# Softmax sums of an attention layer: from TensorE's matmuls to VectorE's turned blocks and transfers

## The chip, the core and the metric

The kernel runs on one core of a Trainium2 chip. The time is the device time in microseconds of one execution. A core has five engines that work side by side, each through its own queue in order: TensorE (PE, matmuls; PEld is its weight load), VectorE (DVE), ScalarE (ACT), GpSimd (POOL) and SyncE (SP), which here only issues transfers (DMAs). TensorE writes to PSUM, eight banks of 128 x 512 f32; the other engines move data between PSUM and SBUF; DRAM is reached by transfers.

## The reference

Two layers follow each other on x of 4 x 1024 x 512 (f32), each with an attention branch s and a feed-forward branch g, and x + s * silu(g) as output. The change touches the attention of layer 1 alone, with 16 heads of 32:

```python
q, k, v = (proj(wq), proj(wk), proj(wv))     # x @ w.T, split into 16 heads of 32
q, k = apply_rope(q, k, sin, cos)
att = jnp.einsum('bhqd,bhkd->bhqk', q, k) * (1.0 / math.sqrt(HD))
att = jax.nn.softmax(att, axis=-1)
y = jnp.einsum('bhqk,bhkd->bhqd', att, v)
y = y.transpose(0, 2, 1, 3).reshape(b, t, c)
return y @ wo.T
```

The softmax divides by the sum over the 1024 keys of the exps. The kernel divides late: it multiplies the undivided y by one over that sum.

## The kernel before, in words

Layer 0 comes first, then layer 1's attention, then layer 1's feed-forward. The attention is cut into 32 units (batch b, group g of four heads, half qh of the queries: 512 queries), in the list `units`; `nu` is 32. Each unit has TB = 8 steps, and one loop over s counts the steps of all units. A step s does two things, for units some way apart:

- for unit s // 8 it finds maxima. `top` (L998) makes scores `sq` of 128 queries with 512 keys for two heads at a time, twice a step, and VectorE reads each `sq` once for its maxima `mx` (L1011). At the unit's last step the maxima are joined, turned (`turn_max`, L1013) and sent by way of DRAM (`turned_d`) to rows `mT`;
- for e = s - 12 (LAG is 12) it weighs. `expo` (L1030) makes the scores `sk` of 128 keys with the unit's 512 queries for four heads, subtracts the maxima by another small matmul (L1043), and ScalarE writes the exps to `pT` (L1048). `weigh` (L1052) multiplies the previous step's `pT` with v into `y`, over the eight steps of a unit. So unit u's exps fall into steps 8u + 12 to 8u + 19.

`exps` (L1063) also adds the eight `pT` of a unit up into `part`, 128 keys x 4 heads x 512 queries: the first add L1077, six more L1079, all on GpSimd. What is left is the sum over the 128 partitions. `total` (L944) does that on TensorE: four matmuls with a matrix of ones (L947) write `z`, where the sum of each query stands in 32 rows, which is how `y` is laid out. It does so at s % 8 == 6 for the unit zu = (s - 6) // 8 - 2, three steps behind that unit's last exp. `divide` (L952) copies `z` from PSUM to `zs` (ScalarE, L956), takes reciprocals (VectorE, four times 128 x 128, L960) and multiplies on GpSimd (L961, `yT` <- `yr`, `zs`). Units 30 and 31 have no full `part`: their sums are built by `total` step by step. When a batch's four groups are divided, `soon` names the step at which its output projection (`wo_out`) joins the work below.

Between these parts, TensorE does slices of longer chains, four `advance` a step: the projections wk, wq and wv of the next group of heads (`heads_in`; their results get the rotary part on VectorE, L919, by transfers `rr` <- `raw`, L916, and on GpSimd, L920 and L921) and the output projection. In a step with `total`, the first of the four comes behind it.

PSUM: `ring` has three tiles of two banks, taken in turn by two `sq` and two `sk` a step, so the second `sk` of a step takes the tile of the step's first `sq`, and the next step's first `sq` the tile of the second; `y` and `acc1` have one bank each, and `acc1` serves `z` and the chains. In SBUF `pT` has three buffers, `part` two, `yr` and `zs` one.

TensorE's instructions run as the code writes them (`manual_schedule` for that engine). The order on the other engines is chosen when the kernel is built, by a scheduler that places an instruction where it reckons that its operands are ready; only what stands in `keep_in_program_order` keeps its place. An engine takes its queue in order: an instruction that waits holds up all behind it.

Of the kernel before, what the change touches and what calls it, by code (L numbers as in the profile page):

```python
# [12 lines left out]
F32 = mybir.dt.float32  # L13
# [3 lines left out]
ALU = mybir.AluOpType  # L17
AX = mybir.AxisListType

P = 128  # L20
B, N, D = 4, 1024, 512
NT = B * N
H, HD = 16, 32
# [12 lines left out]
def kernel(ctx, tc, ins, out):  # L36
    nc = tc.nc
# [3 lines left out]
    dram = ctx.enter_context(tc.tile_pool(name="dram", bufs=1, space=bass.MemoryType.DRAM))  # L41
# [47 lines left out]
    def shared_tile(tag, name):  # L89
        return w0.tile([P, KD, D], F32, tag=tag, name=name)  # L90
# [155 lines left out]
    with ExitStack() as es:  # L246
# [4 lines left out]
        p2 = es.enter_context(tc.tile_pool(name="a0", bufs=2, reuse_waits="tile"))  # L251
# [318 lines left out]
    with ExitStack() as es:  # L570
# [3 lines left out]
        p2 = es.enter_context(tc.tile_pool(name="f0", bufs=2, reuse_waits="tile"))  # L574
# [126 lines left out]
        for g in range(NH0 * NBLK + 2 + 2 * TPB):  # L701
            blk, c = divmod(g, NH0)
            if g == NH0 * NBLK:

                for n in ("wk", "wq", "wv"):
# [3 lines left out]
                            out=W[n], in_=ins[n + "T"].rearrange("(k p) n -> p k n", p=P)  # L709
# [8 lines left out]
            for i in range(TPB):  # L718
                q = g - 2 - 2 * i
# [95 lines left out]
    with ExitStack() as es:  # L815
        wp = es.enter_context(tc.tile_pool(name="a1c", bufs=1, reuse_waits="tile"))
        p2 = es.enter_context(tc.tile_pool(name="a1", bufs=2, reuse_waits="tile"))

        def ring(name):
            return pp.tile([P, 2, 512], F32, tag="ring", name=name, bufs=3)  # L820

        def acc1(name):
            return pp.tile([P, 512], F32, tag="acc1", name=name)

        TB = N // P
# [4 lines left out]
        def load1(b):  # L830
            xnTs[b] = xpair(f"xnT1_{b}")
            for h in range(2):
                load = nc.sync.dma_start(
                    out=xnTs[b][h],
                    in_=xnT_d[b].rearrange("k p n -> p k n")[:, :, h * BLK : (h + 1) * BLK],
                )
                if b:
                    tc.keep_in_program_order(load)
# [7 lines left out]
        turned_d = [  # L846
            dram.tile([8, 512], F32, tag=f"turned{i}", name=f"turned_d{i}") for i in range(2)
        ]

        partner = []  # L850
        for i in range(2):
# [92 lines left out]
        def total(z, part, kb, n):  # L944

            for h in range(4):
                nc.tensor.matmul(  # L947
                    z[h * HD : (h + 1) * HD, :], lhsT=ones[:, :HD], rhs=part[:, h, :],
                    start=(kb == 0), stop=(kb == n - 1),
                )  # L950

        def divide(u, yr, z):  # L952

            b, g, qh = u
            zs = p2.tile([P, 512], F32, tag="zs", name=f"zs_{b}_{g}_{qh}", bufs=1)
            nc.scalar.copy(zs, z)  # L956
            yT = p2.tile([P, 512], F32, tag=f"yT{qh}", name=f"yT_{b}_{g}_{qh}", bufs=5 + qh)
            for c in range(TPB):
                cols = slice(c * P, (c + 1) * P)
                nc.vector.reciprocal(zs[:, cols], zs[:, cols])  # L960
            nc.gpsimd.tensor_tensor(yT, yr, zs, ALU.mult)  # L961
            yTs[b][g, qh] = yT
# [29 lines left out]
        def advance(parts):  # L992
            nonlocal chain
            for _ in range(parts):
                if chain is not None:
                    next(chain)
# [88 lines left out]
        units = [(b, g, qh) for b in range(B) for g in range(4) for qh in range(2)]  # L1085
        nu, LAG = len(units), TB + 4
        yTs = {b: {} for b in range(B)}
# [18 lines left out]
            tc.tile_pool(name="psuma", bufs=1, space=PSUM, reuse_waits="tile")  # L1106
        )
        must, spare = deque(), deque()
        mx, mTs, pTs, ys, parts, lates, soon = {}, {}, {}, {}, {}, {}, {}
        for s in range(TB * nu + LAG + 1):  # L1110

            e = s - LAG
            if s % (2 * TB) == 0 and s < TB * nu:

                assert not must
                n = s // (2 * TB) + 1
                if n < 4 * B:  # L1120
                    b, g = divmod(n, 4)

                    two = (nc.sync, nc.gpsimd) if s == 0 else (nc.sync, nc.sync)
                    must.extend(
                        heads_in(
                            b, g, acc1, {(w, h): two for w in ("wk", "wq") for h in range(2)}
                        )
                    )
                    if g == 3 and b + 1 < B:
                        load1(b + 1)  # L1130
                left = 2
            if s in soon and s < TB * nu:
                spare.extend(wo_out(*soon.pop(s), acc1))
            if s % 2 == 0:

                chain = None
                if spare and left and s < TB * nu:
                    chain = spare.popleft()
                    left -= 1
                elif must:  # L1140
                    chain = must.popleft()
            if s == 2 * TB:
                W["wo"] = shared_tile("wo", "wo")
                tc.keep_in_program_order(
                    nc.sync.dma_start(
                        out=W["wo"], in_=ins["woT"].rearrange("(k p) n -> p k n", p=P)
                    )
                )
            if s % 4 == 0 and s // 4 < TPB:
                lates[s + 2] = s // 4, late(s // 4)  # L1150
            if s < TB * nu:
                u, j = divmod(s, TB)
                if j == 0:
                    mx[u] = p2.tile([P, TPB, 4, 2], F32, tag="mx", name=f"mx_{u}")
                for pair in range(2):
                    top(u, j, pair, mx[u])
                if j == TB - 1:
                    m2 = twice[u % 2][:, :, :8].rearrange("p q (h c) -> p q h c", c=2)

                    w = p2.tile([P, TPB, 4, 2], F32, tag="m1", name=f"m1_{u}")  # L1160
                    nc.vector.tensor_reduce(
                        w[:, :, :, 0], mx.pop(u), AX.X, ALU.max, negate=True
                    )
                    for out, sign in ((w[:, :, :, 1], -1.0), (m2[:, :, :, 0], 1.0)):
                        nc.scalar.activation(
                            out.bitcast(F32R), w[:, :, :, 0], AF.Copy, scale=sign
                        )
                    nc.vector.tensor_reduce(m2[:, :, :, 1], w, AX.X, ALU.add)
            late_exp = s >= TB * nu
            if late_exp:  # L1170
                exps(e)
            if 1 <= e <= TB * nu:
                u, kb = divmod(e - 1, TB)
                if kb == 0:
                    ys[u] = pp.tile([P, 512], F32, tag="y", name=f"y_{u}")
                weigh(u, kb, pTs[e - 1], ys[u])
                if u >= nu - 2:

                    if kb == 0:
                        z_last = acc1(f"z_{u}")  # L1180
                    if u < nu - 1 or kb < TB // 2:
                        total(z_last, pTs[e - 1], kb, TB)
                pTs.pop(e - 2, None)
                if kb == TB - 1:
                    yr = p2.tile([P, 512], F32, tag="yr", name=f"yr_{u}", bufs=1)
                    nc.scalar.copy(yr, ys[u])
                    ys[u] = yr
                    if u == nu - 2:
                        divide(units[u], ys.pop(u), z_last)
                        soon[s] = units[u][0], units[u][2], yTs[B - 1]  # L1190
            held = 0
            zu = (s - 6) // TB - 2
            if s % TB == 0 and 0 < s <= TB * nu:
                turn_max(s // TB - 1)
            if s % TB == 6 and 0 <= zu < nu - 2:
                z = ring(f"z_{zu}")[:, 0, :] if zu == nu - 3 else acc1(f"z_{zu}")
                total(z, parts.pop(zu), 0, 1)
                divide(units[zu], ys.pop(zu), z)
                b, g, qh = units[zu]
                if g == 3:  # L1200
                    soon[s + 4] = b, qh, yTs[b]
            elif s in lates:
                late_turn(*lates.pop(s))
            else:
                held = 1
                advance(1)
            if not late_exp:
                exps(e)
            advance(4 - held)
            if TB * nu - 12 <= s < TB * nu:  # L1210

                nxt = weight(raw1, w0, True)
                if loaded:
                    loaded()
                loaded = nxt
                if s == TB * nu - 1:
                    loaded()

        soon = [*soon.values()]
# [307 lines left out]
```

## Time and profile before

| | |
|---|---|
| median of 3 runs (lowest, highest) | 3093.51 us (3091.0, 3093.84) |
| the profiled execution | 3092.08 us |
| its span, first to last instruction | 3090.2 us |
| TensorE's mean granted clock | 0.996 of full speed |
| `mx` L1011, VectorE, 128 x 1024 | 512 times, 1218 ns each |
| `pT` L1048, ScalarE, 128 x 1024 | 512 times, 1020 ns each |
| `part` L1077 and L1079, GpSimd, 128 x 2048 | 210 times, 4.5 us each |
| `z` L947, TensorE | 33.5 us with `part`, 12.5 us with `pT` |
| `zs` L960, VectorE, 128 x 128 | 128 times, 908 ns each |
| `yT` L961, GpSimd, 128 x 512 | 32 times, 1273 ns each |

How to read the profile: the page gives the busy time of each engine, then the span in 40 slices, in tenths. In groups a line reads: line of the kernel, engine, operation, output <- input, shapes, count | busy time and mean ns | idle time just before, and what ended it. In a timeline a line begins with its start and its length in us, and brackets show how long the engine stood idle before and what released it. SPq is SyncE's queue, where issuing a transfer takes the time shown; its data land later.

### The profile page before, as it was taken

To read this page: it belongs to the slowest core of one execution; us is meant where nothing else is said; L and a number is where in the kernel's file an instruction comes from. 1 tells how busy PE (TensorE), PEld (TensorE's weight loads), DVE (VectorE), ACT (ScalarE), POOL (GpSimd) and SP (SyncE) were. 2 spreads that over 40 slices of the span, in tenths; PEclk is the share of its full clock that TensorE was granted. 3 is DMA by queue.
4 is the path that set the end of the run, shared out by engine and by line. 5 is a ranking of instruction groups with operands and counts; after the bars stand their busy time and mean duration, and the time that the engine had idled before them with its cause. 6 is when DMAs were issued, how large, how long until landed. Compare 5 with 4: busy or idle time off the path is not lost.

```text
span 3090.2 us, 61139 instructions
## 1 busy us (share of the span) xinstructions
PE 3038.3 (98%) x25985; PEld 1730.5 (56%) x25985; DVE 1788.3 (58%) x2569; ACT 1173.7 (38%) x1708; POOL 1557.9 (50%) x742
## 2 busy tenths in 40 slices
PE   9999999999999998999999999999999999999998
PEld 5555555578788873333334444333434436888886
DVE  4444555467777776555555555555555544566655
ACT  3111111145556542444444444444444454333332
POOL 1221212234443444888888988888988940001001
PEclk9999999999999999999999999999999999999999
DMA  4222232323223231100001000100000014222111
GB/s 137 86 86 86 86 86 72 127 96 100 95 92 110 96 129 52 36 9 9 9 18 42 16 10 15 43 16 14 10 18 15 13 46 152 82 69 75 58 52 56
DMA packets 113787, 186.81 MB, mean 60 GB/s; under 512 B 19809, under 2 KB 33633, under 8 KB 113377
## 3 DMA queue, kind: packets, MB, share of 16 engines
q1 hardware_dynamic: 106096, 161.30, 17.3%
q0 software_dynamic: 7280, 21.39, 1.9%
q8 instruction: 205, 3.36, 0.5%
q14 instruction: 78, 0.63, 0.1%
q10 hardware_dynamic: 128, 0.13, 0.0%
HBM read 115.11 MB, written 59.26 MB: 56 GB/s over the span
## 4 chain that ended last, share of the span: by engine, by line
PE 57%; DVE 1%; ACT 1%; POOL 1%; issue 0%; SPq 0%; DMA 0%; ACTq 0%; POOLq 0%; DVEq 0%
PE sk L1037 9%; PE sq L1007 8%; PE y L1056 8%; PE gate L1260 5%; PE up L1260 5%; PE dn L1282 5%; PE wo L862 4%; PE v1ps L862 3%; PE wk L862 3%; PE wq L862 3%; PE sk L1043 2%; PE z L947 1%; ACT pT L1048 1%; DVE zs L960 1%; POOL part L1079 0%; DVE mx L1011 0%
## 5 line engine op out<-in xcount | busy, mean ns | idle before, releaser
L1011 DVE TENSOR_REDUCE mx<-sq 128x2 f32<-128x1024 f32 x512 | 604.2, 1218 | 434.8 <-PE sq L1007 434.0
L1079 POOL TENSOR_TENSOR part<-part,pT 128x2048 f32<-128x2048 f32 x180 | 817.8, 4543 | 17.3 <-ACT pT L1048 8.9
L1048 ACT ACTIVATE pT<-sk 128x1024 f32<-128x1024 f32 x512 | 495.6, 1020 | 557.3 <-PE sk L1043 520.1
L1007 PE MATMUL sq<-wkT,wqT 32*128 32x512 f32 x2048 | 321.0, 639 | 10.0 <-ACT pT L1048 7.0
L1037 PE MATMUL sk<-wqT,wkT 32*128 32x512 f32 x2048 | 322.8, 641 | 0.8 <-DVE mx L1011 0.5
L1056 PE MATMUL y<-pT,v 128*32 128x512 f32 x2048 | 275.5, 608 | 0.1
L1304 POOL TENSOR_TENSOR th<-th,x 128x512 f32<-128x512 f32 x31 | 40.1, 1293 | 458.0 <-DVE th L1303 379.0
L646 PE MATMUL pj<-wpj,hp 128*128 128x512 f32 x1024 | 262.0, 396 | 4.0 <-DVE hp L606 4.0
L593 PE MATMUL fc<-xp,wfc 128*128 128x512 f32 x1024 | 259.0, 395 | 3.6 <-ACT h L598 2.8
L614 POOL TENSOR_TENSOR sums<-sums,h 128x512 f32<-128x512 f32 x112 | 163.1, 1456 | 195.0 <-ACT h L598 189.7
L1043 PE MATMUL sk<-mT,onesr 2*128 2x512 f32 x1024 | 235.7, 788 | 0.0
L382 PE MATMUL qk<-xnT,wqkv 128*128 128x512 f32 x512 | 228.7, 600 | 0.7 <-ACT xnT L156 0.7
L646 PEld LDWEIGHTS pj<-wpj,hp 128*128 128x128 f32 x1024 | 191.2, 188 | 51.9 <-DVE hp L606 10.5
L593 PEld LDWEIGHTS fc<-xp,wfc 128*128 128x128 f32 x1024 | 189.4, 188 | 47.2 <-ACT h L598 6.0
L606 DVE TENSOR_TENSOR hp<-h,hp 128x512 fp32r<-128x512 f32 x128 | 128.2, 1001 | 85.2 <-ACT hp L603 85.2
L1260 PE MATMUL gate<-xp,wf 128*128 128x512 f32 x704 | 174.2, 390 | 0.0
L1260 PE MATMUL up<-xp,wf 128*128 128x512 f32 x704 | 173.9, 389 | 0.0
L1037 PEld LDWEIGHTS sk<-wqT,wkT 32*128 32x128 f32 x2048 | 96.2, 184 | 138.3 <-issue 117.2
L1282 PE MATMUL dn<-wf,hp 128*128 128x512 f32 x704 | 173.6, 390 | 0.0
L1077 POOL TENSOR_TENSOR part<-pT,pT 128x2048 f32<-128x2048 f32 x30 | 136.4, 4548 | 72.1 <-ACT pT L1048 72.0
L1007 PEld LDWEIGHTS sq<-wkT,wqT 32*128 32x128 f32 x2048 | 89.9, 184 | 122.7 <-issue 85.5
L382 PEld LDWEIGHTS qk<-xnT,wqkv 128*128 128x128 f32 x512 | 95.0, 191 | 111.8 <-issue 104.5
(230 smaller groups left out, 4359.3 us busy)
## 6 DMA issues: line engine op xcount, KB each, us to landing
s<-s SPq DMA_DIRECT2D x96, 256.0 KB
xp<-xp_d SPq DMA_DIRECT2D x16, 1024.0 KB
x<-x SPq DMA_DIRECT2D x36, 256.0 KB
x<-in_x SPq DMA_DIRECT2D x32, 256.0 KB
raw_fc<-in_w_fcT SPq DMA_DIRECT2D x32, 256.0 KB
xp_d<-hi POOLq DMA_DIRECT2D x32, 256.0 KB, 2.7
xp_d<-xnT POOLq DMA_DIRECT2D x32, 256.0 KB, 2.9
x0r<-in_x SPq DMA_DIRECT2D x32, 256.0 KB
```

Source lines behind the costliest of these rows:

```text
L382: nc.tensor.matmul(a, lhsT=wqkv[k][:, c0 : c0 + P], rhs=xnTs[blk][:, k, :], start=(k == 0), stop=(k == KD - 1),)
L593: nc.tensor.matmul(a, lhsT=wfc[k][:, c * P : (c + 1) * P], rhs=xp[n][:, k, :].bitcast(F32R), start=(k == 0 and n == 0), stop=(k == KD - 1 ...
L646: nc.tensor.matmul(ds[i], lhsT=hparts[blk, c][n][:, i * P : (i + 1) * P], rhs=wpj[c], start=(c == 0 and n == 0), stop=(c == NH0 - 1 and n ...
L862: nc.tensor.matmul(out[r0 : r0 + HD, :], lhsT=lhsT[:, r0 : r0 + HD], rhs=rhs, start=start, stop=stop,)
L1007: nc.tensor.matmul(sq[:, hh, :], lhsT=qT[r, q0 : q0 + P], rhs=kT[r, n * 512 : (n + 1) * 512], start=True, stop=True,)
L1011: nc.vector.tensor_reduce(mx[:, qt, 2 * pair : 2 * pair + 2, n], sq, AX.X, ALU.max)
L1037: nc.tensor.matmul(sks[h // 2][:, h % 2, :], lhsT=kT[r, kb * P : (kb + 1) * P], rhs=qT[r, qh * 512 : (qh + 1) * 512], start=True, stop=False,)
L1048: nc.scalar.activation(pT[:, 2 * pair : 2 * pair + 2, :], sks[pair], AF.Exp, scale=QKS)
L1056: nc.tensor.matmul(y[r, :], lhsT=v[:, kb, r], rhs=pT[:, h, :], start=(kb == 0), stop=(kb == TB - 1),)
L1079: add.tensor_tensor(parts[u], parts[u], pT, ALU.add)
L1260: nc.tensor.matmul(a, lhsT=ws[n, c][:, k, :], rhs=xp[m][:, k, :], start=(k == 0 and m == 0), stop=(k == KD - 1 and m == 1),)
L1282: nc.tensor.matmul(ds[i], lhsT=hparts[blk, c][n][:, i * P : (i + 1) * P], rhs=w, start=(c == 0 and n == 0), stop=(c == NH1 - 1 and n == 1),)
```

## The change

For units 0 to 29, `z`, its copy to SBUF and the four reciprocals are gone. In their place:

- `sums_of` (eight times a unit): VectorE turns 256 columns of `part` in blocks of 32 x 32, and sums each block's 32 keys (128 x 256 to 128 x 8);
- `gather`: VectorE turns the 128 x 64 sums, a transfer writes them to DRAM (`groups_d`), another reads the four partition groups side by side into `sides`;
- `invert`: VectorE adds the four and takes the reciprocal, of 32 x 64; a transfer writes it to DRAM (`inverse_d`), and four transfers read it back, each spread over 32 partitions, into `zs`;
- `times`: GpSimd multiplies, as before.

The code puts `sums_of` into steps 24 to 27 from the unit's first step, `gather` into step 28, `invert` into 31 and `times` into 34 (before, all was at step 22). `yr` gets a second buffer, the last two units' `zs` takes the tag `mT`, the output projection of a batch joins ten steps later, and eight instead of two of its chains are allowed in the last 16 steps of the loop. The diff, with unchanged parts left out:

```diff
@@ -846,6 +846,10 @@
         turned_d = [
             dram.tile([8, 512], F32, tag=f"turned{i}", name=f"turned_d{i}") for i in range(2)
         ]
+        groups_d = [dram.tile([P, 64], F32, tag=f"groups{i}", name=f"groups_d{i}") for i in range(2)]
+        inverse_d = [
+            dram.tile([2, HD, HD], F32, tag=f"inverse{i}", name=f"inverse_d{i}") for i in range(2)
+        ]
         partner = []
         for i in range(2):
@@ -949,10 +953,61 @@
                     start=(kb == 0), stop=(kb == n - 1),
                 )
+        def sums_of(u, part, c):
+            if c == 0:
+                groups[u] = p2.tile([P, 64], F32, tag="groups", name=f"groups_{u}", bufs=1)
+            t = p2.tile([P, 256], F32, tag="keys", name=f"keys_{u}_{c}", bufs=1)
+            nc.vector.transpose(t, part.rearrange("p h q -> p (h q)")[:, c * 256 : (c + 1) * 256])
+            nc.vector.tensor_reduce(
+                groups[u][:, 8 * c : 8 * c + 8], t.rearrange("p (c a) -> p c a", a=HD), AX.X, ALU.add
+            )
+        def gather(u):
+            back = p2.tile([P, 64], F32, tag="back", name=f"back_{u}", bufs=1)
+            nc.vector.transpose(back, groups.pop(u))
+            at = groups_d[u % 2]
+            nc.sync.dma_start(out=at, in_=back)
+            sides[u] = p2.tile([P, 256], F32, tag="keys", name=f"sides_{u}", bufs=1)
+            nc.sync.dma_start(
+                out=sides[u][:HD, :].rearrange("c (i x) -> c i x", i=4),
+                in_=at.rearrange("(i c) x -> c i x", i=4),
+            )
+        def invert(u):
+            b, g, qh = units[u]
+            inv = p2.tile([P, 64], F32, tag="inv", name=f"inv_{u}", bufs=1)
+            nc.vector.tensor_reduce(
+                inv[:HD, :], sides.pop(u)[:HD, :].rearrange("c (i x) -> c x i", i=4), AX.X, ALU.add
+            )
+            nc.vector.reciprocal(inv[:HD, :], inv[:HD, :])
+            at = inverse_d[u % 2]
+            nc.sync.dma_start(
+                out=at.rearrange("a c b -> c a b"),
+                in_=inv[:HD, :].rearrange("c (a b) -> c a b", a=2),
+            )
+            zss[u] = p2.tile([P, 512], F32, tag="zs", name=f"zs_{b}_{g}_{qh}", bufs=1)
+            for h in range(4):
+                row = at[h // 2, 16 * (h % 2) : 16 * (h % 2) + 16, :]
+                nc.sync.dma_start(
+                    out=zss[u][h * HD : (h + 1) * HD, :],
+                    in_=row.rearrange("c b -> (c b)").partition_broadcast(HD),
+                )
+        def times(u, yr):
+            b, g, qh = units[u]
+            yT = p2.tile([P, 512], F32, tag=f"yT{qh}", name=f"yT_{b}_{g}_{qh}", bufs=5 + qh)
+            nc.gpsimd.tensor_tensor(yT, yr, zss.pop(u), ALU.mult)
+            yTs[b][g, qh] = yT
         def divide(u, yr, z):
             b, g, qh = u
-            zs = p2.tile([P, 512], F32, tag="zs", name=f"zs_{b}_{g}_{qh}", bufs=1)
+            zs = p2.tile([P, 512], F32, tag="mT", name=f"zs_{b}_{g}_{qh}")
             nc.scalar.copy(zs, z)
             yT = p2.tile([P, 512], F32, tag=f"yT{qh}", name=f"yT_{b}_{g}_{qh}", bufs=5 + qh)
             for c in range(TPB):
@@ -1106,6 +1161,7 @@
             tc.tile_pool(name="psuma", bufs=1, space=PSUM, reuse_waits="tile")
         )
         must, spare = deque(), deque()
+        groups, sides, zss = {}, {}, {}
         mx, mTs, pTs, ys, parts, lates, soon = {}, {}, {}, {}, {}, {}, {}
         for s in range(TB * nu + LAG + 1):
@@ -1128,7 +1184,8 @@
                     )
                     if g == 3 and b + 1 < B:
                         load1(b + 1)
-                left = 2
+                left = 2 if n < 4 * B else TB
             if s in soon and s < TB * nu:
                 spare.extend(wo_out(*soon.pop(s), acc1))
             if s % 2 == 0:
@@ -1166,6 +1223,24 @@
                             out.bitcast(F32R), w[:, :, :, 0], AF.Copy, scale=sign
                         )
                     nc.vector.tensor_reduce(m2[:, :, :, 1], w, AX.X, ALU.add)
+            zu, at = divmod(s - 3 * TB, TB)
+            for u, i in ((zu - 1, at + TB), (zu, at)):
+                if 0 <= u < nu - 2:
+                    if i < 4:
+                        for c in (2 * i, 2 * i + 1):
+                            sums_of(u, parts[u], c)
+                        if i == 3:
+                            parts.pop(u)
+                    elif i == 4:
+                        gather(u)
+                    elif i == 7:
+                        invert(u)
+                    elif i == 10:
+                        times(u, ys.pop(u))
+                        b, g, qh = units[u]
+                        if g == 3:
+                            soon[s + 2] = b, qh, yTs[b]
             late_exp = s >= TB * nu
             if late_exp:
                 exps(e)
@@ -1182,24 +1257,16 @@
                         total(z_last, pTs[e - 1], kb, TB)
                 pTs.pop(e - 2, None)
                 if kb == TB - 1:
-                    yr = p2.tile([P, 512], F32, tag="yr", name=f"yr_{u}", bufs=1)
+                    yr = p2.tile([P, 512], F32, tag="yr", name=f"yr_{u}")
                     nc.scalar.copy(yr, ys[u])
                     ys[u] = yr
                     if u == nu - 2:
                         divide(units[u], ys.pop(u), z_last)
                         soon[s] = units[u][0], units[u][2], yTs[B - 1]
             held = 0
-            zu = (s - 6) // TB - 2
             if s % TB == 0 and 0 < s <= TB * nu:
                 turn_max(s // TB - 1)
-            if s % TB == 6 and 0 <= zu < nu - 2:
-                z = ring(f"z_{zu}")[:, 0, :] if zu == nu - 3 else acc1(f"z_{zu}")
-                total(z, parts.pop(zu), 0, 1)
-                divide(units[zu], ys.pop(zu), z)
-                b, g, qh = units[zu]
-                if g == 3:
-                    soon[s + 4] = b, qh, yTs[b]
-            elif s in lates:
+            if s in lates:
                 late_turn(*lates.pop(s))
             else:
                 held = 1
```

## The prediction

> **What bounds the kernel now.** The page comes first. TensorE is busy for 98% of the span, and in the stretch that the change touches (layer 1's attention, about 1160 to 2577 us) GpSimd shows eights and nines as well:
>
> ```profile
> PE 3038.3 (98%) x25985; PEld 1730.5 (56%) x25985; DVE 1788.3 (58%) x2569; ACT 1173.7 (38%) x1708; POOL 1557.9 (50%) x742
> POOL 1221212234443444888888988888988940001001
> L1079 POOL TENSOR_TENSOR part<-part,pT 128x2048 f32<-128x2048 f32 x180 | 817.8, 4543 | 17.3 <-ACT pT L1048 8.9
> ```
>
> So there are two engines with little to give: TensorE, which has none, and GpSimd, which spends 7 x 4.55 = 31.8 us a unit on `part` alone. A unit (8 steps) takes 43.3 us: the last `part` adds of units 0 and 29 end at 1260.5 and 2516.6 us, 29 units apart.
>
> The second view is the timeline of some steps. I call S(n) the start of step n's first `sq`:
>
> ```profile
> 1804.69 1.14 PE L1007 MATMUL sq<-wkT,wqT 32*128 32x512 f32 x8
> 1805.87 0.69 DVE L919 TENSOR_TENSOR wqT<-wq,cs 128x512 f32<-128x512 f32 x1 [2.88 <-ACT raw_wq L911]
> 1806.48 2.35 DVE L1011 TENSOR_REDUCE mx<-sq 128x2 f32<-128x1024 f32 x2
> 1807.75 0.19 PEld L1037 LDWEIGHTS sk<-wqT,wkT 32*128 32x128 f32 x2 [0.26 <-DVE mx L1011]
> 1809.00 1.94 ACT L1048 ACTIVATE pT<-sk 128x1024 f32<-128x1024 f32 x2 [3.16 <-PE sk L1043]
> 1810.47 1.14 PE L1007 MATMUL sq<-wkT,wqT 32*128 32x512 f32 x8
> ...
> 1826.76 1.14 PE L1007 MATMUL sq<-wkT,wqT 32*128 32x512 f32 x8
> ...
> 1828.71 1.04 PE L947 MATMUL z<-part,ones 128*32 128x512 f32 x8
> ...
> 1830.51 3.39 DVE L960 RECIPROCAL zs<-zs 128x128 f32<-128x128 f32 x4 [0.22 <-ACT zs L956]
> ...
> 1832.87 1.14 PE L1007 MATMUL sq<-wkT,wqT 32*128 32x512 f32 x8
> ...
> 1837.18 0.31 DVE L1016 STREAM_TRANSPOSE mt<-m 128x128 f32<-128x128 f32 x1
> 1837.52 3.11 SPq L1023 DMA_DIRECT2D turned_d<-mt  x4
> 1842.08 1.13 SPq L1026 DMA_DIRECT2D mT<-turned_d  x4
> ```
>
> A plain step takes 5.24 us. The first step shown takes 5.78, because VectorE's L919 stood ahead of `mx` and the second `sk` pair waits for the ring tile which `mx` has to read: 0.6 us of VectorE delay costs TensorE 0.5 us. VectorE has slack as a share and almost none ahead of an `mx`. The step with `z` takes 6.11, so `z` is worth 0.87 us.
>
> The third view is GpSimd alone. It is strictly in order: after a unit's first add comes the division of the unit before, and only then the other adds:
>
> ```profile
> 1743.73 4.54 POOL L1077 TENSOR_TENSOR part<-pT,pT 128x2048 f32<-128x2048 f32 x1
> 1748.24 1.26 POOL L961 TENSOR_TENSOR yT<-yr,zs 128x512 f32<-128x512 f32 x1
> 1749.46 27.69 POOL L1079 TENSOR_TENSOR part<-part,pT 128x2048 f32<-128x2048 f32 x6
> 1782.95 4.54 POOL L1077 TENSOR_TENSOR part<-pT,pT 128x2048 f32<-128x2048 f32 x1 [5.80 <-ACT pT L1048]
> ```
>
> **The order of the changed program.** TensorE's order is written by hand; VectorE's, GpSimd's and SyncE's are the scheduler's. The built program has on VectorE, for unit 17 (the others alike, in four early units one `mx` sooner):
>
> ```
> mx sq_19_4_0 | 1 pair: transpose part_17, reduce | mx sq_19_4_1 | 7 pairs | back_17
> mx sq_19_5_0 | mx sq_19_5_1 | inv_17: reduce of sides_17, reciprocal | mx sq_19_6_0
> ```
>
> The text puts the pairs at steps 24 to 27 behind a unit's start and `inv` at 31. The program has all of them within steps 20 to 22: one burst, whose head waits for GpSimd's last add, and then a wait for two transfers, each ahead of an `mx`. GpSimd's order is unchanged: first add, `yT`, six adds. `yT` now waits for the transfers of `zs`.
>
> **What goes.** `z` (30 x 0.87 = 26 us of TensorE), four reciprocals of 0.9 us and a copy of 0.59 a unit. These would be the gain.
>
> **What comes, from T0, the end of a unit's last add.** T0 is never early: unit 12's add ends at 1777.2, 5.5 us behind S(116) = 1771.7, its step 20, and `mx` of that step's second pair would end at S + 3.5. So `sq` of step 21 waits in every unit.
>
> 1. The burst. A transpose of 128x128 takes 0.31 (L1016), so 128x256 takes between 0.31 and 0.62; with a base like L1161's 0.19 for 32 elements I take 0.44. The reduce of 256 lies between 0.19 (L1161) and 0.68 (L1327, 512): 0.42. Each pair's two results are waited for; L1168 to L1016 shows a 0.1 us gap. A pair: 0.44 + 0.42 + 0.2 = 1.06 (ends 0.5 and 1.5). Eight pairs 8.5, `mx` 1.2, `back` 0.3: 10.0 us (ends 5.6 and 13.5). `mx` of sq_5_0 ends at T0 + 11.2.
> 2. TensorE goes on with step 21's second `sk` pair. In the row above, 2.8 us pass from the end of `mx` (1807.66) to the next step: step 22 at T0 + 14.0.
> 3. The clock. The busy times of two stretches ahead of the attention's steady part (first TensorE's, the clock third from the end):
>
> ```profile
> 1160.00:1165.00 5.00, 2.79 (x28) 1.30 (x32) 4.38 (x9) 1.26 (x2) 3.44 (x5) 0.87 0.25 68
> 1165.00:1170.00 5.00, 5.00 (x64) 2.08 (x60) 2.69 (x3) 0.06 (x1) 1.69 (x2) 0.79 0.00 0
> ```
>
> TensorE is idle for 2.2 of the first 5 us, and then, all busy, granted 0.79. If the granted clock halves, the two make (0.13 + 0.21) x 5 / 0.5 = 3.4 us of it, which cost 1.7 us of work. Here stalls of some 5 us come in every unit; I add 1.7 (ends 0 and 3.4): T0 + 15.7.
> 4. Steps 22 to 27: 6 x 5.24 + 0.6 for L919 = 32.0; the last exp ends 0.7 into the next step, the add takes 4.6: next T0 at T0 + 53.0. This is TensorE's circle.
> 5. GpSimd's circle. `mt` to `turned_d` to `mT` gives the transfer: issues of 0.66 to 0.8, and 1.45 from the last issue's end (1840.63) to the reader. One leg is 2.1 (ends 1.6 and 3.5). Two legs: `sides` at T0 + 14.2; `inv` 0.42 + 0.45 + 0.1, done at 15.2; its write 17.3; four broadcasts, issued by 20.0, and 1.45: `zs` at 21.4; `yT` (1.27) ends at 22.7; six adds 27.3: T0 + 50.0, plus 2.55 for each rotary pair (L920, L921) among them.
> 6. SyncE's queue. In 11 units a rotary pair stands right behind `yT`, and its eight transfers are issued behind `zs`: 20.0 + 5.4 (eight issues at 0.67) + 1.45 = 26.8. With one more pair the unit is 59.2 us, with two more 61.8.
>
> By the program's order 18 units have no or one pair (50.0 or 52.6, under TensorE's 53.0), 4 have two, 7 have three: 18 x 53.0 + 4 x 59.2 + 7 x 61.8 = 1623 us where before has 1256: +367. The last burst holds up step 254: it began 1.9 us behind T0 and now 15.7, +13.8, less 3 for `z` and the reciprocals there (that step took 8.16) and 2.5 because the last steps before it take 4.6 instead of 5.24: +8. Sum +375. Against the profiled execution's own 3092.1 (span 3090.2 and 1.9 around it) that is 3467; the median of the runs is 1.4 higher: **3468 us**.
>
> The Trainium skill, "TensorE: Matmul & The Clock Gate", Part 1, says that an idle window of about 3.4 us halves the clock until one busy window has passed. The trace shows a lower clock after 2.2 us of idleness already. By the page a stall at each burst costs at least one window, 1.7 us, as I took; a window is free-running, so a second can fall in, and the sum would be some 50 us higher. The page thus speaks against a change that makes TensorE stop regularly.
>
> What I cost at nothing: `keys`, `back` and `zs` have one buffer each, but their readers are done a whole unit earlier. `yr` has two now, and the ACT copy waits for nobody. The seven added transfers move about 0.3 MB a unit over DMA engines that are 4% busy in 1300 to 1400.
>
> **The rivals.**
> (a) The burst alone counts; the transfers come out shorter, and GpSimd waits for nothing that TensorE's circle doesn't hide. Then all 29 units are 53.0: +281 + 8, 3382. For it: GpSimd also stands still until step 21's exp (T0 + 14.4). Against it: `yT` stands ahead of six adds that need 27.3.
> (b) The transfers are dear, 3.5 a leg: four legs add 5.6 to GpSimd's circle, 55.6, 58.2, 64.8 and 67.4: 1755, so 3600. For it: sixteen `rr` issues in one queue take 17 us, over 1 us each.
> (c) The change half works: `part` is ready when asked and a pair costs near 0.5: about 5 us a unit, 3245. Against it: T0 above.
> (d) It isn't slower: the pairs fall into VectorE's 2.9 us pauses behind `mx` and the transfers into steps that nobody waits for. Then `z` is the whole effect, 3093.5 - 26 = 3067. It decides as soon as T0 comes before S(20) + 3.5 and the pairs stand apart; the trace has T0 at 5.5 at the earliest and the order has them together.
>
> **How the numbers follow.** Forecast 55%, (a) 20%, (b) 16%, (c) 6%, (d) 3%. With every cost at its low end (burst 5.6, no clock loss, legs of 1.6) the units are 46.9 to 55.4 us and the time 3289; with every high end 59.1 to 70.9 and 3702. Not all ends come together, so the range leaves out the outer part of both: 3320 to 3610. About 0.2%, 6 us, is what a measurement can tell from no change: faster 3% (d), within 0.2% 1%, slower 96%.
>
> **What would show it.** Right: VectorE's first transpose waits for `part` some 3 us or more in each unit and the pairs run in one block of 7 to 10 us; TensorE waits for `mx` L1066 twice a unit, 8 to 15 us together; GpSimd waits for `zs` ahead of `yT`; the clock in the attention falls under 1.00; units are 53 to 62 us apart. Wrong: `part` ready when VectorE comes to it, `yT` with no wait, or the granted clock unmoved, which takes some 50 us off. If units are near 44 us apart, the order's meaning has been misread.

## The result and the profile after

| | before | after |
|---|---|---|
| median of 4 runs (lowest, highest) | 3092.26 us (3086.34, 3093.84) | 3482.13 us (3479.46, 3492.0) |
| the profiled execution | 3092.08 us | 3479.97 us |
| its span | 3090.2 us | 3478.1 us |
| TensorE's mean granted clock | 0.996 | 0.937 |

The changed kernel takes 1.1271 times as long, with an interval of 1.1243 to 1.1298. The forecast was 3468 us.

The page of after first: the busy times, GpSimd and the granted clock in 40 slices, and the two groups in which the waits of VectorE and TensorE show (behind the last bar: idle time ahead of the group, and what ended it).

```profile
PE 3187.7 (92%) x25745; PEld 1769.4 (51%) x25745; DVE 1930.1 (55%) x3019; ACT 1159.8 (33%) x1678; POOL 1559.0 (45%) x742
POOL 1212112344344476767576767666676762000001
PEclk9999999999999997879698989889888989999999
L965 DVE STREAM_TRANSPOSE keys<-part 128x256 f32<-128x256 f32 x240 | 106.5, 444 | 217.1 <-POOL part L1134 211.0
L1062 PE MATMUL sq<-wkT,wqT 32*128 32x512 f32 x2048 | 367.2, 719 | 144.6 <-DVE mx L1066 137.9
```

TensorE has lost its 98%, GpSimd its eights and nines: neither engine is kept busy any more. GpSimd does what it did before. TensorE does 240 matmuls less and is nevertheless busy for 149 us more: the clock falls in just the stretch that was changed. VectorE waits 211 us for `part`, TensorE for VectorE's `mx`.

One unit in the timeline of after. T0, the end of the unit's last add, is 1944.56:

```profile
1944.59 0.45 DVE L965 STREAM_TRANSPOSE keys<-part 128x256 f32<-128x256 f32 x1 [2.99 <-POOL part L1134]
...
1946.68 1.14 PE L1062 MATMUL sq<-wkT,wqT 32*128 32x512 f32 x8 [2.18 <-DVE mx L1066]
...
1953.07 0.24 DVE L972 STREAM_TRANSPOSE back<-groups 128x64 f32<-128x64 f32 x1
1953.24 2.32 DVE L1066 TENSOR_REDUCE mx<-sq 128x2 f32<-128x1024 f32 x2
...
1954.48 1.22 PE L1092 MATMUL sk<-wqT,wkT 32*128 32x512 f32 x2 [4.17 <-DVE mx L1066]
...
1956.59 0.59 DVE L984 TENSOR_REDUCE inv<-sides 32x64 f32<-32x256 f32 x1 [1.03 <-DMA sides<-groups_d]
...
1958.69 4.53 POOL L1132 TENSOR_TENSOR part<-pT,pT 128x2048 f32<-128x2048 f32 x1 [14.13 <-ACT pT L1103]
...
1963.18 1.29 POOL L1004 TENSOR_TENSOR yT<-yr,zs 128x512 f32<-128x512 f32 x1
```

The first transposition waits for `part`; the `mx` behind it releases TensorE's next `sq` 2.2 us late. The other pairs then stand in one block until `back` at 1953.07; TensorE waits 4.2 us more, and GpSimd 14.1 us for the exp that TensorE delays. When GpSimd has done its next first add, `zs` has arrived: `yT` waits for nothing here. The same waits of after between 1300 and 2800 us (us in all, times, longest):

```profile
DVE keys L965 <- POOL part L1134: 197.2, 27, 15.2
PE sq L1062 <- DVE mx L1066: 126.6, 23, 9.7
PE sk L1092 <- DVE mx L1066: 96.1, 26, 11.1
POOL part L1132 <- ACT pT L1103: 323.2, 26, 14.8
```

The lengths of all steps show where the time went. I added them up from the starts of the first `sq` of steps 16 to 255 (30 units), by a step's place in its unit (s mod 8), as differences from before:

| kernel | place 0 | 2 | 4 | 5 | 6 | all eight |
|---|---|---|---|---|---|---|
| after | -0.5 | +1.8 | **+185.1** | **+200.4** | +2.8 | +389.6 |
| e3, block held later | **+200.1** | +1.6 | +7.4 | +6.5 | -22.3 | +198.1 |
| e4, one pair, no transfers | -3.5 | +1.8 | **+181.6** | +52.4 | -16.5 | +218.8 |
| e5, no transfers | -3.5 | +1.8 | **+182.3** | **+224.4** | -1.3 | +401.0 |
| e2, division where it stood | -0.5 | +1.9 | +1.7 | **+138.3** | -7.7 | +133.7 |
| e1, all held | -3.6 | +6.6 | +2.0 | +10.3 | -22.1 | -9.9 |
| e7, `yr` three | +4.6 | +4.4 | +1.8 | 0.0 | -21.2 | -13.4 |
| e8, inverse sooner | +3.7 | +1.9 | +1.7 | -0.1 | -17.2 | -13.1 |

(Places 1, 3 and 7 differ by under 4 us, in e3 place 1 by 7.4.) The two profiled executions are 387.9 us apart, so all of the loss lies in these steps: half at place 4, where VectorE waits for `part`, half at place 5, where the block stands.

Not all of it is standing still. Steps 16 to 255 of e1, which does the same work, and of after (length, TensorE's busy time, and its granted clock third from the end):

```profile
1228.80:2515.30 1286.50, 1275.09 (x15418) 505.42 (x15414) 837.70 (x1171) 544.32 (x683) 1120.68 (x349) 1.00 0.11 28
1226.70:2912.80 1686.10, 1441.03 (x15416) 551.64 (x15414) 858.83 (x1192) 547.34 (x683) 1122.36 (x350) 0.88 0.08 22
```

After is 400 us longer there. TensorE is idle for 245 us instead of 11, which is 234 of them. By the trace's clock records, 317 us of its busy time fall on half clock, in e1 6; if work takes twice as long there, that is some 156 us. The two are nearly the whole loss. At place 5 TensorE is idle for only 65 us, and busy at half clock for 227. By the same reckoning e3, e4 and e2 have 119, 167 and 60 us more of idleness than e1, and 78, 73 and 70 us by the clock. This is an account of the traces; no run has the stalls at full clock.

### The profile page after: what moved, and what is told of

The parts are those of the page before. It is cut to its first block, busy times and chain, and to the rows that moved or that the text cites. A ratio compares the mean times of both kernels' runs of the same rounds, so it can differ in the third digit from the quotient of the medians.

```text
span 3478.1 us, 61412 instructions
## 1 busy us (share of the span) xinstructions
PE 3187.7 (92%) x25745; PEld 1769.4 (51%) x25745; DVE 1930.1 (55%) x3019; ACT 1159.8 (33%) x1678; POOL 1559.0 (45%) x742
## 4 chain that ended last, share of the span: by engine, by line
PE 39%; POOL 9%; DVE 8%; SPq 3%; issue 3%; DMA 2%; ACT 1%; POOLq 0%; ACTq 0%; DVEq 0%
POOL part L1134 8%; PE sk L1092 6%; PE sq L1062 5%; PE gate L1327 5%; PE up L1327 5%; PE dn L1349 4%; PE y L1111 4%; PE wo L866 3%; DVE keys L965 3%; DVE groups L966 3%; SPq L920 3%; DVE mx L1066 2%; PE v1ps L866 2%; PE wk L866 2%; PE sk L1098 1%
## 5 line engine op out<-in xcount | busy, mean ns | idle before, releaser
L1062 PE MATMUL sq<-wkT,wqT 32*128 32x512 f32 x2048 | 367.2, 719 | 144.6 <-DVE mx L1066 137.9
L1092 PE MATMUL sk<-wqT,wkT 32*128 32x512 f32 x2048 | 389.6, 679 | 104.5 <-DVE mx L1066 104.2
L1111 PE MATMUL y<-pT,v 128*32 128x512 f32 x2048 | 300.6, 660 | 0.1
L1098 PE MATMUL sk<-mT,onesr 2*128 2x512 f32 x1024 | 275.0, 823 | 0.0
L1092 PEld LDWEIGHTS sk<-wqT,wkT 32*128 32x128 f32 x2048 | 112.6, 194 | 271.2 <-DVE mx L1066 148.1
L1062 PEld LDWEIGHTS sq<-wkT,wqT 32*128 32x128 f32 x2048 | 100.9, 205 | 270.4 <-DVE mx L1066 149.9
L965 DVE STREAM_TRANSPOSE keys<-part 128x256 f32<-128x256 f32 x240 | 106.5, 444 | 217.1 <-POOL part L1134 211.0
```

The costliest lines, as they stand in the source:

```text
L1062: nc.tensor.matmul(sq[:, hh, :], lhsT=qT[r, q0 : q0 + P], rhs=kT[r, n * 512 : (n + 1) * 512], start=True, stop=True,)
L1092: nc.tensor.matmul(sks[h // 2][:, h % 2, :], lhsT=kT[r, kb * P : (kb + 1) * P], rhs=qT[r, qh * 512 : (qh + 1) * 512], start=True, stop=False,)
L1098: nc.tensor.matmul(sks[h // 2][:, h % 2, :], lhsT=onesr[r, :], rhs=mTs[u][r, :].bitcast(F32R), start=False, stop=True,)
L1111: nc.tensor.matmul(y[r, :], lhsT=v[:, kb, r], rhs=pT[:, h, :], start=(kb == 0), stop=(kb == TB - 1),)
```

## The experiments

**The theory (place).** The added work costs nothing by its amount; it costs because the built order puts it ahead of an `mx`, for which TensorE waits. **Rivals:** the amount of work on VectorE (A), or the transfers (T). `keep_in_program_order` holds an instruction behind all that the code wrote before it for its engine, so it undoes the scheduler's moves one by one. Diffs are against after, where nothing else is said.

**e1: all of it held at the steps where the code writes it.**

```diff
-            nc.vector.transpose(t, part...)
-            nc.vector.tensor_reduce(groups[u]...)
+            tc.keep_in_program_order(nc.vector.transpose(t, part...))
+            tc.keep_in_program_order(nc.vector.tensor_reduce(groups[u]...))
```

and likewise for `back`, `inv`, its reciprocal and `yT`.

> The changed kernel with the pairs, the turn back, the inverse and the division held at the steps where the code puts them (24 to 27, 28, 31 and 34); same work, same transfers. In the built order no two pairs stand ahead of an mx that is due, and the division stands behind five or six adds of a later unit. Theory P, place: the loss comes from where VectorE's instructions stand, ahead of the next mx, and from their wait for GpSimd's last add; here nothing is left of it and z is saved: 3092 less 26, less 5 for the five early units whose reciprocals held up an mx, plus up to 8 where a rotary part now delays step 6: 3055 to 3085, about 3068. Rival A, amount: VectorE's 16 added instructions a unit cost their 7 us wherever they stand: over 3250. Rival T, transfers: two detours through DRAM hold GpSimd and SyncE up as before: over 3400.

Measured: 3096.22 us (3086.88 to 3105.19), ratio to before 1.0009 [0.9996, 1.0021]. VectorE in two steps of e1 (the lines are two further down in this kernel):

```profile
1653.61 2.36 DVE L1068 TENSOR_REDUCE mx<-sq 128x2 f32<-128x1024 f32 x2 [1.03 <-PE sq L1064]
1655.88 0.43 DVE L966 STREAM_TRANSPOSE keys<-part 128x256 f32<-128x256 f32 x1
1656.35 0.42 DVE L968 TENSOR_REDUCE groups<-keys 128x8 f32<-128x256 f32 x1
1656.80 0.45 DVE L966 STREAM_TRANSPOSE keys<-part 128x256 f32<-128x256 f32 x1
1657.28 0.42 DVE L968 TENSOR_REDUCE groups<-keys 128x8 f32<-128x256 f32 x1
1658.84 2.36 DVE L1068 TENSOR_REDUCE mx<-sq 128x2 f32<-128x1024 f32 x2 [1.14 <-PE sq L1064]
```

The same eight pairs, two to a step, fit between the `mx` of one step and the next and leave 1.14 us over. The 386 us are gone with all the work and all seven transfers still there: A and T fall as causes. Of the 26 us of `z` that I expected beyond that, 22 come, at place 6: where a turned chain (L923) falls into the step without `z`, it takes 5.77 instead of 6.20 us, since that delay was hidden behind `z` before. But place 5 loses 10 us again, because ScalarE's `yr` copy now waits for a buffer that `yT` reads, up to 4.7 us; and place 2 loses 7, of them 4.9 in one step near the end, where ScalarE waits 4.2 us for the transfer of a weight. The table is made from profiled executions, and e1's is the fastest of its 12; the median is 9 us above it. One of the ten waits of the `yr` copy in the timeline of e1:

```profile
1722.68 0.58 ACT L1263 COPY yr<-y 128x512 f32<-128x512 f32 x1 [4.63 <-POOL yT L1006]
```

**e3: only the division held** (`inv`, reciprocal and `yT`, by the three lines that e2 lacks). With nothing of the unit's division to place sooner, the scheduler leaves all eight pairs together, behind an `mx` where `part` has long been ready. So this run has the block without the wait for `part`.

> Only the inverse and the division are held (steps 31 and 34); the eight pairs stay one block, but the scheduler now puts it behind the last mx of step 23, where part has been ready for some 4 us or more. Theory P: the wait for GpSimd's last add is gone, the block is left: 1.1 for the inverse and 7.5 for the pairs from 3.5 us into the step end at 12.1, the next mx was due at 6.4: TensorE stops 5.5 us a unit, and the clock costs it some 2 more: 30 x 7.5 = 225 over the first kernel, 3230 to 3310, about 3280. A rival that puts all on the wait for part: about 3070 as the first. Rival T: the transfers are off VectorE's and GpSimd's way here too, so about 3070 as well.

Measured: 3300.17 us, 1.0662 [1.0646, 1.0679], 204 over e1. TensorE's longest wait for `mx` ahead of the second `sk` pair is under half of after's 11.1 us, as the waits show (us in all, times, longest):

```profile
PE sk L1092 <- DVE mx L1066: 75.8, 18, 5.1
```

The table shows the block where it now stands: +200 at place 0, as much as at place 5 in after. Eight pairs of 0.93 us cost nothing spread out and 6.9 us a unit in one piece (200 over 29 units), the half clock that follows the stall included.

**e4: the scheduler's order, one pair a unit, no transfers.** Only the first 256 columns of `part` are summed, and the division multiplies by a constant.

```diff
-                groups[u] = p2.tile(...)
+                groups[u] = all_groups      # one tile for all units
+            else:
+                return                      # sums_of: pairs 1 to 7
-            nc.sync.dma_start(out=at, in_=back)   # and the other six transfers
+            sides[u] = back
-            nc.vector.reciprocal(inv[:HD, :], inv[:HD, :])
+            nc.vector.reciprocal(inv[:HD, :], sides.pop(u)[:HD, :])
+            zss[u] = fixed
```

> The changed kernel, scheduler's order, with one pair instead of eight and no transfers (only the first 256 columns of part are summed; the division multiplies by a constant). What is left at step 20 is the wait for part and, behind it, 0.9 + 1.2 (mx) + 0.2 + 0.5 of VectorE before the next mx. Theory P: mx of step 21 ends some 4.2 us behind the last add instead of 11; units of TensorE's circle 51.0 - 6.9 - 1 (clock) = 43 and of GpSimd's some 47, about 45.5 on average: 3482 - 29 x 10.9 = 3166, 3120 to 3220. A rival by which the wait itself is free: about 3075. Rival T: the transfers were the loss: about 3075 too, so this run tells the wait from nothing, and the next one the transfers.

Measured: 3311.12 us, 1.0711 [1.0696, 1.0727]: far above my 3166. The wait for `part`, with next to no work behind it, costs 215 us over e1. The waits of VectorE and TensorE in e4, in the same columns:

```profile
DVE keys L972 <- POOL part L1121: 196.8, 28, 12.9
PE sq L1049 <- DVE mx L1053: 127.7, 24, 9.1
```

I had taken T0 at 5.4 us behind S(20), the earliest. That holds for the units without rotary work among GpSimd's adds, where place 4 takes 7.48 us; with three rotary pairs T0 comes 12.5 to 12.8 us behind S(20), and place 4 takes 14.6 to 14.9. Before, T0 lay 5.3 to 13.9 us behind S(20) too, but TensorE ran on and let GpSimd fall behind by those 8.6 us; one transposition ahead of an `mx` ties it to GpSimd's lateness.

The 52 us at place 5 of e4 are the clock's: TensorE isn't idle there at all, and 116 us of that place run at half clock, which makes some 58; the stall at place 4 leaves it behind. The same eight matmuls of `sq` and of `y` right behind such a stall and one step later:

```profile
1944.85 2.09 PE L1049 MATMUL sq<-wkT,wqT 32*128 32x512 f32 x8 [8.93 <-DVE mx L1053]
1946.86 1.94 PE L1098 MATMUL y<-pT,v 128*32 128x512 f32 x8
...
1951.99 1.14 PE L1049 MATMUL sq<-wkT,wqT 32*128 32x512 f32 x8
1953.07 1.06 PE L1098 MATMUL y<-pT,v 128*32 128x512 f32 x8
```

One thing more differs: with no `zs` to wait for, the scheduler puts `yT` ahead of the first add in nearly all units here and in e5, in after behind it.

**e5: the scheduler's order, all eight pairs, no transfers.** The division multiplies by a constant; the four partition groups are not added. The diff is e4's without the change in `sums_of`.

> The changed kernel, scheduler's order, all eight pairs, no transfers (the inverse is taken of one part of the sums, without the detour; the division multiplies by a constant). Theory P: the block and its wait stay at step 20, TensorE's circle stays at 51 to 52 us; GpSimd has no zs to wait for, and the rotary transfers no longer stand behind zs in SyncE's queue: the eleven long units lose 4 us and more: 3360 to 3440, about 3400. Rival T: GpSimd's wait for zs and VectorE's for sides were most of it: under 3250.

Measured: 3502.16 us, 1.1329 [1.1312, 1.1345], not the 3400 expected, and even a little above after. The waits of e5, for `part` and for `mx` ahead of the second `sk` pair, are much those of after, where the first is 197.2 us and the second 96.1:

```profile
DVE keys L968 <- POOL part L1117: 184.7, 26, 12.9
PE sk L1075 <- DVE mx L1049: 105.9, 26, 9.6
```

So taking after's transfers out gains nothing. Place 5 has 24 us more than in after (the other places 13 less): here the reciprocal of 0.54 us stands ahead of the second `mx`, in after behind it. That is read from the trace and not tried by a run.

**e2: pairs and `back` held, the division left to the scheduler.** It is e1 less three holds, and the scheduler puts `inv` right behind `back`, ahead of an `mx`.

```diff
-            tc.keep_in_program_order(nc.vector.tensor_reduce(inv...))
-            tc.keep_in_program_order(nc.vector.reciprocal(inv...))
-            tc.keep_in_program_order(nc.gpsimd.tensor_tensor(yT...))
+            (the three as in after)
```

> As the first, but the inverse and the division are left to the scheduler: the inverse stands right behind the turn back at step 28, so VectorE waits there for two transfers, and the division stands behind the last add of the next unit. Theory P: the two legs took 3.3 us in the changed kernel (end of back to start of inv); from mx's end 3.5 us into the step that gives 3.5 + 0.3 + 3.2 + 1.1 = 8.2 us, where the next mx is due at 6.4: 1.7 us a unit, 51 over the first kernel: 3095 to 3160, about 3120. Rival A: over 3250 as before. Rival T: the wait at its worst place, in line, so about as slow as the changed kernel, over 3350.

Measured: 3231.92 us (3215.39 to 3239.21), 1.0441 [1.0412, 1.0469], against 3120 expected. The mechanism was as expected, its size wasn't. One unit in the timeline of e2:

```profile
1774.90 12.96 SPq L920 DMA_DIRECT2D rr<-raw_wq  x11
...
1785.39 0.23 DVE L974 STREAM_TRANSPOSE back<-groups 128x64 f32<-128x64 f32 x1
...
1787.95 0.39 SPq L976 DMA_DIRECT2D groups_d<-back  x1
...
1791.06 0.33 SPq L978 DMA_DIRECT2D sides<-groups_d  x1
1792.81 0.58 DVE L986 TENSOR_REDUCE inv<-sides 32x64 f32<-32x256 f32 x1 [7.19 <-DMA sides<-groups_d]
```

`back` is done at 1785.62, but its write is issued 2.3 us later, when the rotary part's sixteen issues in SyncE's queue are through (1787.86; the line has the last eleven), and the read follows that issue after 3.1 us, where it is 1.5 in after. From the end of `back` to `inv` it is 7.2 us here and 3.3 in after. So transfers do cost TensorE time as soon as VectorE waits for them ahead of an `mx`: 136 us over e1, about half of it by the clock. In after SyncE's queue is free when `back` ends, behind the wait for `part` and the block; that these two are what lets the transfers hide there is read from the trace and not tried by a run.

**e6: the small edits alone.** Before, with the two buffers of `yr`, the tag `mT`, the output projection ten steps later and the eight chains at the end; `z` and `divide` as they were.

```diff
-                left = 2
+                left = 2 if n < 4 * B else TB
-                    yr = p2.tile([P, 512], F32, tag="yr", name=f"yr_{u}", bufs=1)
+                    yr = p2.tile([P, 512], F32, tag="yr", name=f"yr_{u}")
```

> The kernel before with the small edits alone: yr with two buffers, zs under the tag mT for all units, the output projection of a batch ten steps later, eight of its chains allowed in the last sixteen steps. The sums stay on TensorE. All theories: within 6 us of 3092, since no wait in the trace of before is for yr or zs, and the chains are the same work. If it is off by more, part of the change's time belongs to these edits.

Measured: 3095.39 us, 1.0009 [1.0, 1.0018]. They have no part in the loss.

**e7: e1 with three buffers of `yr`** (`zs` takes the tag `xn`, for room).

```diff
-                    yr = p2.tile([P, 512], F32, tag="yr", name=f"yr_{u}")
+                    yr = p2.tile([P, 512], F32, tag="yr", name=f"yr_{u}", bufs=3)
-            zss[u] = p2.tile([P, 512], F32, tag="zs", ...)
+            zss[u] = p2.tile([P, 512], F32, tag="xn", ...)
```

> The first experiment (all held at the code's steps) with a third buffer for yr; zs moves to the tag of a tile that is used only in the first steps, for room. In the first experiment's trace ScalarE waited for yT before its copy to yr ten times, up to 4.7 us, and the step with it took 6.4 to 6.8 instead of 5.3 in nine units. Theory P: 9 x 1.3 = 12 us less, so about 3084 and under the kernel before, 3072 to 3090. If a reader of yr is not the cause: 3096 again.

Measured: 3087.86 us (3081.57 to 3097.36), 0.9992 [0.9982, 1.0002]. Place 5 is back at 0.0, as expected; most of it comes back at place 0 (+4.6 where e1 has -3.6), where an exp waits for a `pT` that GpSimd's late add still reads.

**e8: e7 with `invert` at step 30 instead of 31.**

```diff
-                    elif i == 7:
+                    elif i == 6:
                         invert(u)
```

> The held version with three buffers of yr, and `invert` at step 30 instead of 31, so that the five transfers from the inverse to zs are issued while SyncE's queue is free, and not between the maxima's transfers and the next unit's rr <- raw_wk. In the version with invert at step 31 GpSimd waits 3.4 us for that rr in the units with three rotary pairs, its eight issues begin 1.8 us later behind zs than behind the maxima's transfers, and in nine units the first step of the following unit takes 6.4 us instead of 5.24 because an exp waits for a pT buffer that GpSimd's late add still reads. Theory: the queue makes GpSimd late; then that first step goes back to 5.24 in the nine units, some 10 us less: 3078 us, 3072 to 3086. Rival: GpSimd is late because three rotary pairs and seven adds simply fill the unit (7 x 4.55 + 3 x 2.55 + 1.27 = 40.8 of 43.6 us), and the queue only moves the idle time; then the time stays at 3084 to 3092.

Measured: 3082.87 us (3076.66 to 3092.33), 0.9968 [0.9957, 0.9979]: the one version that beats both kernels. The time is in the theory's range, but the theory isn't what happened. Place 0 still has +3.7 where e7 has +4.6. `zs` is out of the way of `rr`, but now three issues of `mT` stand ahead of it, and GpSimd waits longer for the same `rr`. GpSimd's timeline in e7 and then in e8, at the same place (in e8 the trace puts the end of the wait down to the fourth `mT`, issued right behind the eight `rr`):

```profile
1706.29 1.28 POOL L924 TENSOR_TENSOR rr<-rr,cs 128x512 f32<-128x512 f32 x1 [3.37 <-DMA rr<-raw_wk]
```

```profile
1708.48 1.26 POOL L924 TENSOR_TENSOR rr<-rr,cs 128x512 f32<-128x512 f32 x1 [4.58 <-DMA mT<-turned_d]
```

So the rival is right for the steady units: the queue only moves GpSimd's idle time. The gain over e7 in the profiled runs, 3.1 us, lies behind step 255, where a wait of 3.6 us of TensorE's `y` for `pT` is gone. The two were not timed side by side, so that e8 is better than e7 is likely and not shown; that it is better than before is.

## Why the prediction was right, point by point

The place of the loss, both stalls and the end result were as predicted: 3482 against 3468 us, slower. Most steps were right within 1 or 2 us; that the sum came so close is luck in part, since errors of opposite sign cancelled.

- **Step 1, the burst.** `mx` of sq_5_0 was put at T0 + 11.2; it ends at 9.9 in the unit above. A pair is 0.93 us instead of 1.06 (0.444 and 0.42, with gaps of 0.04 instead of 0.1).
- **Steps 2 and 3, the next step and the clock.** 2.8 and 1.7 were predicted from the end of `mx` to S(22); it is 5.2 (1954.4 to 1959.63), so the clock takes some 2.4 in this unit. The busy times of the engines and TensorE's granted clock around that moment (third from the end):

```profile
1949.00:1954.00 5.00, 1.30 (x12) 0.30 (x4) 4.69 (x11) 0.00 (x0) 0.00 (x0) 0.89 0.00 0
1954.00:1959.00 5.00, 4.52 (x28) 1.83 (x32) 2.68 (x4) 1.94 (x2) 0.31 (x1) 0.50 0.07 15
```

  TensorE is busy for 1.3 of the first 5 us, and when it has work again, it gets half its clock for the whole of the next 5. The clock records add up to 438 us at half speed in after and 27 in before. The Trainium skill, "TensorE: Matmul & The Clock Gate", Part 1, gives windows of about 3.4 us for both directions; the records of this trace last 3.41 us or a whole multiple of it, but for the last. The page asks for an idle window of that length; here the clock fell at 1952.9 us, when TensorE had been idle for 2.6 of the 3.4 us before. S(22) is thus at T0 + 15.1 instead of 15.7. The unit shown has 6.8 us of half clock; other pieces last up to 41 us. Over all steps the 156 us above make 5.2 a unit, so the term of 1.7 was too small by two thirds. No run separates the clock from the stall that brings it.
- **Step 4, TensorE's circle of 53.0 us.** It sets the light units, as predicted: 51.0 to 52.6. But those with one rotary pair behind `yT` take 55 to 57 (one 62): GpSimd waits some 3 us ahead of `rr`, since, as the trace reads, that transfer can't start before TensorE's delayed chain ends. The prediction let a pair cost GpSimd its 2.55 us and no wait; GpSimd's waits ahead of `rr` come to 85 us in 1300 to 2800. This is the part that was too low.
- **Step 5, the transfers.** Too dear. From T0: `inv` starts at 12.0 instead of 14.2, the reciprocal ends at 13.2 instead of 15.2, `yT` ends at 19.9 instead of 22.7. An issue takes 0.33 us, or 0.42 for the four into `zs`, not the 0.66 to 0.8 of `turned_d`. What `yT` waits for is no longer `zs` but the add ahead of it. Of after's waits in 1300 to 2800:

```profile
POOL yT L1004 <- DMA zs<-inverse_d: 9.9, 11, 1.8
```

  The forecast that GpSimd's circle would run through the wait for `zs` was wrong, and rival (a) right on that one point. GpSimd waits for the exp that TensorE's stall delays (323.2 us, 26 times, ahead of the first add), so the transfers lie beside that wait; in e5, without them, nothing is gained.
- **Step 6, SyncE's queue.** Units with two pairs were put at 59.2 and take 57.1 to 59.8; with three, 61.8 and 60.2 to 62.3.
- **The sum.** 29 units take 1635.5 us by T0, +379 against the predicted +367; what is left of the 387.9 between the profiled runs, 8 us, is the size of the term for the end. That term gave step 254 of before 8.16 us; from its first `sq` to the next it takes 6.30 (2518.55 to 2524.85), so that its size fits is chance. Transfers and burst too dear, clock and `rr` too cheap.
- **`z`.** The circle of six steps of 5.24 counted its loss as a gain. Place 6 has +2.8 in after, where e1 has -22: the half clock reaches into that step, which takes 5.25 to 8.2 us there; TensorE isn't idle in it, and 69 us of it run at half clock. Rival (d) had 26 us as the whole effect, 3067; e1 is (d)'s case, built, and it gives 3096, and e8 3083. A step that loses an instruction gains less than that instruction's price where another delay was hidden behind it.

The experiments put numbers on the two halves, over e1: wait for `part` alone +215 (e4), block alone +204 (e3), both +386 (after). They add up to 33 us more than both together, and either alone would have made the change a loss of 7%.

Two things stay open: how much of the clock's 156 us would come back as waiting if the clock stayed up, and why the times of e1 spread over 18 us in 12 runs, and those of e7 over 16, where before's spread over 13 in 23. The slow ones go with a lower mean granted clock (e1: 0.996 at 3087 to 3089 us, 0.990 to 0.992 at 3102 to 3105), which names no cause.

## What to carry to other kernels

Work for an engine with slack is free only if it stands in the slack: ask ahead of which instruction it lands in the built order, and who waits for that instruction. An instruction that waits for a late engine, put into an in-order queue ahead of one that feeds the bottleneck, carries the whole lateness over, however short it is itself. A stall of TensorE cost more here than its own length: to 234 us of idleness came some 156 us by the half clock that followed. Where a scheduler chooses the order, read the order it built, and hold what it moves too early: here holding six kinds of instruction was worth 386 us, and with one more buffer and the inverse one step sooner a loss of 12.7% became a gain of 0.3%.

## What the runs showed of the hardware

- The same DRAM detour (one write, one read, 128 x 64) took 3.3 us from the producer's end to the reader where SyncE's queue was free, and 7.2 us behind the last of sixteen issues of another transfer.
- A transposition of 128 x 256 in 32 x 32 blocks took 0.444 us, one of 128 x 64 0.24; eight dependent pairs on VectorE followed each other with gaps of 0.04 us.
- One stall of 2.2 and one of 4.2 us of TensorE within 8 us brought the granted clock to 0.50 for the next 5 us. At half clock eight matmuls of `sq` (32 x 512 each) took 2.09 us, and 1.14 at full clock.
